# A convolution by transforms on one core: two products moved by a quarter of a row, and DRAM pitches off 4096 bytes

## The chip, the cores and the metric

The kernel runs on one core of a Trainium2 chip. The core has five engines that run side by side, each through its own list of instructions in order: PE (TensorE, matrix products; its weight loads are listed as PEld), DVE (VectorE), ACT (ScalarE), POOL (GpSimd) and SP (SyncE, which here only issues DMA transfers). POOL and ACT issue some transfers too. The transfers are carried by 16 DMA engines. Engines wait for each other with semaphores.

The metric is the device time of one execution in microseconds (us). The kernel before took 16473.95 us, the median of three runs (16464.4 to 16498.5).

## The reference

The input x has four images of 512 x 512 positions with 16 channels. Two layers follow each other, each with a group normalization in front and an addition of its own input behind:

```
x = x + conv_by_transform(gn(x), h0, numerators, denumerator)
x = x + cosine_conv_3x3(gn(x), kernel, bias, radius)
```

The first layer is a two-dimensional filter as long as the image. For each pair of an input and an output channel a rational function (numerator over denominator, 8 x 8 coefficients) gives a frequency response, from which a response of 512 x 512 taps is made. Each image, padded to 1024 x 1024, is transformed, multiplied at every frequency with the 16 x 16 matrix of that frequency, and transformed back; the first 512 x 512 positions are kept. The second layer is a 3 x 3 convolution divided by the norm of its window, with an arccosine and a hyperbolic tangent of the norms. All is in float32.

## The kernel before, in words

The work runs in four stages, one after the other.

- *filter_phase* makes the matrices of the frequencies along the width and stores them in the DRAM tensors g_d, four of them with 128 rows each. A row holds, for 128 places along the height, 16 output channels j with 8 x 16 numbers each: 8 KB per place.
- *forward_phase* transforms x along the width and stores it in x_d (four tensors, 128 rows of 256 KB).
- *conv_phase* takes one row, that is one frequency along the width, after the other: 513 steps of the same kind, since the first frequency is done in two. Within a row it transforms along the height, mixes the channels, and transforms back. The results go to y_d (four tensors, 128 rows of 256 KB).
- *last_phase* transforms y_d back along the width (the inverse), and then does the second layer.

The change is in conv_phase and in the pitches of g_d, x_d and y_d. A row n goes through conv_phase in five steps, so step(n) works on five rows at once:

- `load_x(n + 3)`, `load_g(n + 2)`, `load_xe(n + 1)`: SP issues the loads. x is 256 KB, g is 1 MB. xe comes in two transfers of 1.5 MB (line 814), read back from the small DRAM buffers xf_d in a shifted form.
- `turn_x(n + 3)` prepares the coefficients dfs_n of one row: one ACT instruction (763) and one DVE instruction (765).
- `x_part(n + 2, m)` for the four images m: the transform of x along the height, one product on PE per image (776, two matmuls each in the trace) into the PSUM tile px, which takes two images. After the second and the fourth, `evict` copies px into the first part of xe.
- `x_late(n + 2)`: POOL issues the store of xe to xf_d (790), multiplies xe with turning factors (four products in 797, then 798) and adds (799) to get xl, and stores xl (790). Behind it `half_shift` lets ACT copy one half of xe and one half of xl into another part of xe (808). The second of these copies needs xl.
- `g_part(n + 1, j)`: the transform of g along the height on PE (828), 16 channels j, into the PSUM tiles pg, and from there by `evict` into gh. There are three such tiles, and a quarter of a row takes two.
- `mix(n, g)`: the product over channels on PE (844), from xe and gh into pm, and from there by `evict` into yf.
- `over_q(n - 1, t)`: the first inverse step. PE transposes yf into pz (865), ACT copies one half out as zq (872), and DVE does five operations (873 to 877) that give z. After the last, POOL makes zd and z of it (881, 883).
- `over_g(n - 2, m)` for m from 0 to 3: the last inverse step on PE (902, four matmuls per m in the trace) from z and zd into the PSUM tile py. After m = 3 it is copied to yo, which POOL stores to y_d (913).

`evict` gives every third copy to DVE (726) and the others to ACT (728), in the order in which the program calls it. The tiles px, pz and py share three PSUM buffers. The tile xe has three buffers in SBUF; g, x, gh, yf and z have two each, and xl has one.

A step has four quarters, k = 0 to 3. Each does eight `mix` groups, four `g_part`, four `over_q`, and what the diff below shows. The calls only give the program order; the layer that records the program then places each engine's instructions, so the order on one engine may differ a little from that of the calls. SP's own order is x, xe, g, xe, in every row.

In g_d, x_d and y_d a row has PITCH floats added behind it. The helper `dram(t, row, offset, *dims)` builds the access: the row pitch comes from the tensor's shape, the rest from the call.

## Time and profile before

| what | value |
|---|---|
| median of three runs | 16473.95 us |
| the profiled execution's own time | 16489.29 us |
| its span in the profile | 16487.4 us |
| granted PE clock, mean | 0.972 |
| busy: PE, DVE, POOL, ACT | 91%, 64%, 62%, 54% of the span |
| DMA moved | 4542.92 MB, 276 GB/s on average |
| SP's queue (q1) | 67.9% of the time of 16 DMA engines |
| POOL's queue (q0) | 9.5% |
| stages, from the windows of the trace | filter to about 3560 us, forward to 4600, convolution to 13610, inverse to 14560, the rest to the end |

The page gives averages over stages of different kinds, so what a change in conv_phase is worth has to be read from that stage. A group of instructions has its line number, its engine, and the tiles that it writes and reads. In a list of waits "A <- B" says that A's engine stood idle until B released it; "issue" is a wait with no semaphore that the profile shows. A busy PE is not PE at its peak, because the ends of matmuls are modelled. An instruction of PE in float32 shows as two in the trace.

### The profile page before, as it was taken

Reading aid. Unit: us, or ns where it says so; the run is one execution under the profiler, and the core shown is the slowest. Engines: PE = TensorE matmul, PEld = TensorE weight load, DVE = VectorE, ACT = ScalarE, POOL = GpSimd, SP = SyncE. Lnnn points to the kernel's source line nnn. Section 1 sums busy time; section 2 is a strip of 40 time slices with the busy share of each in tenths; the row PEclk is TensorE's granted clock in tenths of the full one; section 3 lists DMA queues with packets and bytes.
Section 4 is the critical chain, followed back from the end, with each engine's and each line's share of the span. In section 5 each row is a group of like instructions: output and inputs, shape, how many; then the busy total and the mean of one; then the engine's idle time right before and its main releaser. Section 6 shows DMA issues by size and latency. Waiting matters only on the chain. (4 is left out here: it accounts for less than half of the span.)

```text
span 16487.4 us, 538106 instructions
## 1 busy us (share of the span) xinstructions
PE 15039.9 (91%) x232588; PEld 11221.5 (68%) x232588; DVE 10549.6 (64%) x20763; ACT 8870.6 (54%) x17007; POOL 10203.4 (62%) x9645
## 2 busy tenths in 40 slices
PE   7999999999988889898988899888889998988898
PEld 5555555554567777677777777777777777777787
DVE  8999999974545555555555555555555552447877
ACT  4666666653345555555555555555555551027888
POOL 7777777763356666666666666666666660237766
PEclk8999999999999999999999999999999999989999
DMA  4888888888888888888888888888888886885531
GB/s 139 241 244 247 240 243 248 240 244 250 251 282 328 324 326 330 317 327 329 328 329 317 326 328 327 317 318 324 324 326 329 326 321 232 313 279 167 167 110 67
DMA packets 2914640, 4542.92 MB, mean 276 GB/s; under 512 B 126114, under 2 KB 2094460, under 8 KB 2801422
## 3 DMA queue, kind: packets, MB, share of 16 engines
q1 hardware_dynamic: 2703070, 3836.37, 67.9%
q0 software_dynamic: 172336, 605.00, 9.5%
q10 hardware_dynamic: 36864, 67.13, 1.2%
q8 instruction: 1833, 30.03, 0.7%
q14 instruction: 537, 4.40, 0.1%
HBM read 3030.71 MB, written 1477.31 MB: 273 GB/s over the span
## 5 line engine op out<-in xcount | busy, mean ns | idle before, releaser
L828 PE MATMUL pg<-c_dg,g 64*128 64x128 f32 x32832 | 2838.7, 290 | 344.4 <-ACT gh L728 192.2
L844 PE MATMUL pm<-xe,gh 128*32 128x64 f32 x131328 | 2380.2, 222 | 520.0 <-issue 299.3
L844 PEld LDWEIGHTS pm<-xe,gh 128*32 128x32 f32 x131328 | 2001.1, 110 | 1113.6 <-issue 891.7
L828 PEld LDWEIGHTS pg<-c_dg,g 64*128 64x128 f32 x32832 | 2277.5, 189 | 690.3 <-issue 248.1
L873 DVE TENSOR_TENSOR z<-zq,pz 128x256 f32<-128x256 f32 x2052 | 859.5, 419 | 2634.6 <-ACT zq L872 2567.4
L726 DVE COPY gh<-pg 128x512 f32<-128x512 f32 x2046 | 1408.2, 688 | 1208.9 <-PE pg L828 1205.8
L458 PE MATMUL pt<-ev_in,c_todd 128*128 128x512 f32 x4096 | 1927.5, 609 | 16.2 <-DMA ev_in<-g_d 16.2
L797 POOL TENSOR_TENSOR xu<-xe,c_late 128x256 f32<-128x256 f32 x2052 | 1391.7, 702 | 808.5 <-ACT xe L728 791.2
L388 DVE RECIPROCAL dn<-dn 128x256 f32<-128x256 f32 x1024 | 1722.8, 1724 | 17.6
L728 ACT COPY yf<-pm 128x512 f32<-128x512 f32 x2046 | 1211.4, 592 | 886.9 <-PE pm L844 873.2
L389 POOL TENSOR_TENSOR sp<-m,dn 128x512 f32<-128x512 f32 x1024 | 1300.9, 1271 | 592.4 <-DVE dn L388 552.0
L808 ACT COPY xe<-xl 64x1024 f32<-64x1024 f32 x513 | 538.7, 1050 | 1877.9 <-POOL xl L799 1877.8
L728 ACT COPY gh<-pg 128x512 f32<-128x512 f32 x2058 | 1200.2, 583 | 368.8 <-PE pg L828 365.7
L865 PE MATMUL pz<-c_ident,yf 128*128 128x128 f32 x8208 | 1371.7, 290 | 24.2 <-issue 10.8
L458 PEld LDWEIGHTS pt<-ev_in,c_todd 128*128 128x128 f32 x4096 | 728.2, 190 | 920.6 <-issue 792.3
L417 ACT COPY st<-pg 128x256 f32<-128x256 f32 x2048 | 616.8, 391 | 1301.5 <-PE pg L406 1301.3
L406 PEld LDWEIGHTS pg<-c_dinv,sp 64*128 64x128 f32 x16384 | 1005.5, 196 | 442.2 <-ACT sp L394 232.6
L799 POOL TENSOR_TENSOR xl<-xl,xu 128x1024 f32<-128x1024 f32 x513 | 1209.5, 2358 | 40.2
L406 PE MATMUL pg<-c_dinv,sp 64*128 64x128 f32 x16384 | 1108.2, 287 | 60.2 <-ACT sp L394 44.6
L881 POOL TENSOR_TENSOR zd<-z 128x512 f32<-128x512 f32 x513 | 653.7, 1274 | 765.4 <-DVE z L873 765.3
L1279 PE MATMUL pc<-l_band,xn 128*128 128x160 f32 (+2 forms) x6144 | 1076.2, 333 | 51.7 <-DVE e_o L1334 51.7
L913 POOL DMA_DIRECT2D y_d<-yo x511 | 296.5, 580 | 1325.0 <-ACT yo L728 1299.8
(211 smaller groups left out, 30193.2 us busy)
## 6 DMA issues: line engine op xcount, KB each, us to landing
xe<-xf_d SPq DMA_DIRECT2D x1026, 1536.0 KB
g<-g_d SPq DMA_DIRECT2D x511, 1024.0 KB
g_d<-st SPq DMA_DIRECT2D x256, 1024.0 KB
ev_in<-g_d SPq DMA_DIRECT2D x1024, 256.0 KB
g_d<-ot SPq DMA_DIRECT2D x1024, 256.0 KB
xf_d<-xe POOLq DMA_DIRECT2D x513, 448.0 KB, 8.2
xf_d<-xl POOLq DMA_DIRECT2D x513, 448.0 KB, 5.4
x_d<-xo SPq DMA_DIRECT2D x128, 1024.0 KB
```

The costliest lines, as they stand in the source:

```text
L388: nc.vector.reciprocal(dn, dn)
L389: nc.gpsimd.tensor_mul(w["sp"][:, v], w["m"][:, v], bc(dn, 2, [P, 2, 2, P]))
L406: nc.tensor.matmul(pg[u][:, n, k].rearrange("p a x -> p (a x)"), w["sp"][q, n, k, c, :], dinv[q, 2 * kp + k, c, :], start=(c == 0), stop=( ...
L458: nc.tensor.matmul(pt, todd[:, c, kc, hh * P : hh * P + P], ev[:, kc, c], start=(kc == 0), stop=(kc == 1),)
L726: nc.vector.tensor_copy(dst, src)
L728: nc.scalar.copy(dst, src)
L797: nc.gpsimd.tensor_mul(u[:, :, h, c], xe[:, :, h, 1 - c], bc(late[:, 1 + c], 2, [P, F, 2]))
L799: nc.gpsimd.tensor_add(xl.rearrange("p f h c k -> p (f h c k)"), xl.rearrange("p f h c k -> p (f h c k)"), u.rearrange("p f h c k -> p (f ...
L828: nc.tensor.matmul(pg[c][:, j % 4], g[half, j], dg[half], start=True, stop=True)
L844: nc.tensor.matmul(pm[32 * q : 32 * q + 32, g % 8], gh[:, f].rearrange("p c j -> p (c j)"), xe[:, :, f].rearrange("p t h c k -> p t (h c k ...
L865: nc.tensor.transpose(pz[:, t % 4].rearrange("p v q x -> p (v q x)"), y[:, at].rearrange("p g x -> p (g x)"), ident)
L1279: nc.tensor.matmul(pc[:, lo:hi, :].rearrange("p w j -> p (w j)"), xns[q][:, h * P + dh : h * P + dh + P], bands[dh][:, o : o + hi - lo, :] ...
```

## The change

The order of the quarters changes in three places. `x_part` of two of the four images is called at the end of the fourth quarter of the step before, the other two stay at the end of the first quarter, ahead of `x_late`. `turn_x` is called in the second quarter instead of the third. `over_g` is called for two m in the second quarter and for two in the third, instead of for all four in the third.

The pitches change as well. A place of g takes 8 KB + 512 bytes (GP = 2176 floats) instead of 8 KB; G_ROW follows. PITCH goes from 1024 to 1152 floats, so that rows of g_d, x_d and y_d have 4.5 KB added instead of 4 KB. The places where g is stored (424), read back and stored (444, 464) and loaded (735, 738) follow the new pitch. The bytes that are moved and the length of each piece stay as they were.

```diff
+GP = C * 8 * C + 128
-G_ROW = 2 * S * C * 8 * C
+G_ROW = P * GP
-PITCH = 1024
+PITCH = 1152
...
-                            out=dram(g_d[h], None, a * G_ROW // 2 + ((32 * q + 16 * kp) * C + j) * 8 * C,
-                                     [C * 8 * C, 16], [1, 8 * C]),
+                            out=dram(g_d[h], None, a * G_ROW // 2 + (32 * q + 16 * kp) * GP + j * 8 * C,
+                                     [GP, 16], [1, 8 * C]),
...
-                return [((first[c] + 4 * (tb % 8)) * C + j) * 8 * C for c in range(2)]
-
-            step = [C * 8 * C, 4], [1, 8 * C]
+                return [(first[c] + 4 * (tb % 8)) * GP + j * 8 * C for c in range(2)]
+
+            step = [GP, 4], [1, 8 * C]
...
-                nc.sync.dma_start(out=t, in_=dram(g_d[rc], r, 0, [w, P], [1, w]))
+                nc.sync.dma_start(out=t, in_=dram(g_d[rc], r, 0, [GP, P], [1, w]))
...
-                    nc.sync.dma_start(out=t[to : to + 32], in_=dram(g_d[rc], r, at * w, [w, 32], [1, w]))
+                    nc.sync.dma_start(out=t[to : to + 32], in_=dram(g_d[rc], r, at * GP, [GP, 32], [1, w]))
...
                 if row(2) and k == 0:
-                    for m in range(B):
+                    for m in range(2, B):
                         x_part(n + 2, m)
                     x_late(n + 2)
                 if row(2) and k >= 2:
                     half_shift(n + 2, k - 2)
-                if row(3) and k == 2:
+                if row(3) and k == 1:
                     turn_x(n + 3)
-                if row(-2) and k == 2:
-                    for m in range(4):
-                        over_g(n - 2, m)
+                if row(3) and k == 3:
+                    for m in range(2):
+                        x_part(n + 3, m)
+                if row(-2) and k in (1, 2):
+                    for m in range(2):
+                        over_g(n - 2, 2 * (k - 1) + m)
```

## The prediction

> **What bounds the kernel now.** I read the page first (its chain of work that ended last is spread so thin over 538106 instructions that every entry rounds to 0%), then a table of busy time by stage. Columns: stretch in us, its length, busy us and instructions of PE, PEld, DVE, ACT and POOL, granted PE clock, share of the 16 DMA engines, GB/s.

> ```profile
> 0.00:3560.00 3560.00, 3475.22 (x29921) 2086.21 (x29922) 3328.98 (x3022) 2180.03 (x4860) 2636.11 (x2215) 0.98 0.80 231
> 4600.00:13610.00 9010.00, 8073.24 (x184035) 6436.62 (x184033) 4908.87 (x13272) 4771.32 (x8704) 5779.41 (x5639) 0.98 0.87 324
> 13610.00:14560.00 950.00, 841.16 (x4319) 725.11 (x4320) 335.09 (x928) 99.32 (x258) 142.49 (x64) 0.95 0.78 279
> ```

> The filter (first line) keeps PE busy 98% and hardly waits for DMA. The convolution (second) is 55% of the span; PE stands idle 10% of it, no engine is full, DMA is nearly so. The program order of its 513 rows repeats, so one row is the unit: from the first to the last row of the trace, 17.53 us each. Who waits there (us in total, times, longest, in 6000 to 13000 us, 400 rows):

> ```profile
> ACT xe L808 <- POOL xl L799: 1467.6, 399, 6.5
> PE pm L844 <- issue: 225.5, 225, 3.7
> PE pg L828 <- ACT gh L728: 152.9, 167, 3.8
> PE pm L844 <- DMA xe<-xf_d: 53.4, 50, 2.7
> ```

> ACT waits 3.7 us in every row for POOL's xl; the evictions of gh queue behind it, and PE behind those. The timeline of one row shows the loop (start, length, engine, line, operation):

> ```profile
> 6456.27 1.10 PE L844 MATMUL pm<-xe,gh 128*32 128x64 f32 x64 [0.39 <-ACT zq L872]
> ...
> 6460.60 1.36 POOL L797 TENSOR_TENSOR xu<-xe,c_late 128x256 f32<-128x256 f32 x2 [1.41 <-ACT xe L728]
> ...
> 6460.70 1.10 PE L844 MATMUL pm<-xe,gh 128*32 128x64 f32 x64
> ...
> 6461.10 0.68 DVE L726 COPY xe<-px 128x512 f32<-128x512 f32 x1
> ...
> 6462.08 0.56 POOL L790 DMA_DIRECT2D xf_d<-xe  x1
> ...
> 6466.02 2.36 POOL L799 TENSOR_TENSOR xl<-xl,xu 128x1024 f32<-128x1024 f32 x1
> ...
> 6468.41 1.06 ACT L808 COPY xe<-xl 64x1024 f32<-64x1024 f32 x1 [3.73 <-POOL xl L799]
> ...
> 6469.97 0.59 ACT L728 COPY gh<-pg 128x512 f32<-128x512 f32 x1
> ...
> 6470.62 1.16 PE L828 MATMUL pg<-c_dg,g 64*128 64x128 f32 x14 [1.08 <-ACT gh L728]
> ...
> 6472.38 0.68 DVE L726 COPY gh<-pg 128x512 f32<-128x512 f32 x1
> ...
> 6473.17 1.04 PE L844 MATMUL pm<-xe,gh 128*32 128x64 f32 x60 [0.39 <-ACT zq L872]
> ```

> Row to row it is 6473.17 - 6456.27 = 16.90 us. I count from T = 6460.70, the start of the second quarter (the end of x_part): xl is done at T+7.68, half_shift ends at 8.77, gh of the third quarter is out at 9.86, PE resumes at 9.92, the last gh is out at 12.36 (DVE first has five operations on z, released by ACT's zq), the next row's mix starts at 12.47 and its own second quarter 4.43 later: 16.90. In the trace 216 of 507 rows take up to 16.96 us; the others are longer, 0.63 on average over all. PE's own work without waits, summed from the usual length of each of its groups, is 14.96 us.

> Two things lengthen rows. One is PE "issue" stalls of about 1 us at no semaphore. The other is the load of xe (rows in which the mix starts 0.58 us after the last packet): by the trace's single packets this load ends 15.03 us (the median of 407 loads) after its issue, which in turn stands 5.42 us after xl is done (the store has to land).

> [...] gh and zq, long ready, stand 3.73 us behind L808. [...] POOL's stores and SP's loads share the time, at 87% here. [...] In 6000 to 13000 us there are 1131 packets of 16 KB on the instruction queue, 2.8 per row, and half of the PE gaps inside a group end within 1.45 us after one of them: not wholly hidden here.

> **The change part by part.** No instruction is added or removed. As built, POOL and SP keep their order; on PE two of four x_part products (4 of 8 matmuls in the trace) go from the end of the first quarter to the end of the fourth, before the next mix, and half of over_g goes from the third quarter to the second. DVE takes one yf in place of one gh. turn_x moves a quarter earlier: 0.52 us ACT and 0.55 us DVE, in slots where both wait (ACT idle 3.7 us); free, and without cover 0.5 us.

> *First quarter.* mix 1.03 + g 1.09 + transposes 0.59 + half x_part 0.91 = 3.62 us instead of 4.43 (before pulled one pair of g ahead of mix, after does not).

> *xl.* First-half xe is out before POOL has finished zd and z (they end near T-0.8), so POOL takes its first two products at once; it no longer idles 1.41. But the second half still comes at the end of the first quarter. DVE evicts it behind one z operation that waits for ACT's zq, near T-0.1: 0.25 to 0.93, against 0.40 to 1.08. POOL's store issue starts at 1.0 instead of 1.38; from there 6.30 to the end of xl (6468.38 - 6462.08): T+7.30. So 0.38 is won, not the whole 1.41.

> *The stall.* PE is in the fourth quarter at the same T as before: two quarters of 1.03 + 1.09 + 0.59 + 0.94 = 7.3. half_shift ends at 8.39, yf and gh bring 9.48, PE resumes at 9.54 (9.92 before); about 0.95 us of stall stays.

> *Into the next row.* g ends at 10.6, transposes 0.59, the moved half of x_part 0.91: PE is free at 12.1. zq at 9.76 lets DVE start; 1.6 for z, 0.68 for gh: 12.0. So mix starts near 12.15, and what was an idle gap and part of a stall now holds 0.91 of work. Row: 12.15 + 3.62 = 15.77 by engines alone. over_g's first half waits for DVE's eviction of px (0.93) and stands at 2.7: no wait. The moved x_part waits for yo (ACT, 10.25) and for x, issued a row earlier: none.

> *The load.* Issue at 7.30 + 5.42 = 12.72; plus 15.03 and 0.58: 28.33, which must equal 12.15 + one row: 16.18. Before, the same sum gives 7.68 + 5.42 + 15.61 - 12.47 = 16.24, hidden under 16.90; with the engines at 15.77 the load is the next thing late. Fast rows are then 16.2.

> *Stretching.* I keep 0.45 of the 0.63 for PE's own stalls (the rest I give to late loads), and add 0.10 since the spread of the load counts fully: 16.75. That is 0.78 per row, by 513 rows: -400 us.

> *Pitches.* All byte and packet counts stay. Packets of g take 345 ns on average (309 median), of xe, whose rows stand at 4.5 KB already, 177 (159): both 11% over, so a pitch off 4096 does not mark xe out. x stands at 85 (84), the 512-byte packets of the filter at 28.5 (27), and there PE hides them. I take 0. Ends: all of g's excess gone is 36 ns x 128 / 16 = 0.29 us of the load, -150 us; a loss of the same size is not excluded.

> The profiled execution took 16489.29 us (span 16487.4), 15 above the median of the runs shown. 16489 - 400 = 16089; on the median, **16074 us**.

> **Rivals.** *DMA holds more of it.* DMA works 0.87 x 17.53 = 15.2 us per row; at 16.75 that is 91%. If stores and loads now collide, the load grows by 0.4 and rows take 17.2: -170, 16300 us. For it: the share; against: the load kept to 15 us throughout. *The load is not in the way.* Shorter packets of g or earlier stores let the engine loop through: 15.8 + 0.45 = 16.25, -650, 15820 us. Against it: 16.18 above. *Slower.* Places 8.5 KB apart make g's reads slower, and these run between the two halves of xe's load. At 12.72 + L + 0.58 - 12.15 + 0.45 = 17.53 the load decides: L = 15.93, 0.9 us more, or 112 ns on each of g's packets. At half as long again (+173 ns, L = 16.4) it is +240 us, 16710. Against: the padded xe. *It doesn't do what it says:* if POOL still starts late, only x_part's place counts, rows near 16.9 to 17.5; that falls among the first rival or no change.

> **How the numbers follow.** Forecast 0.50 (15950 to 16200), DMA holds more 0.20 (16200 to 16430), load not in the way 0.17 (15750 to 15950), no change 0.04, slower 0.09. A measurement here tells about 0.2% from no change. Range 15820 to 16440 leaves about 2 in 10 out: half of the low case, no change and slower. Faster 0.87, same 0.04, slower 0.09.

> **What would show it.** In the convolution: rows near 16.2 at the fast end; POOL's wait for the first xe gone; ACT's wait at half_shift still above 2.5 us a row; PE's wait for gh in the fourth quarter near 1 us; more PE wait for DMA at mix; DMA share above 0.90; g packets near 345 ns; filter and inverse unmoved. It is wrong if fast rows stay at 16.9 (the loop is another), go to 15.8 (the load gave way), or if g's packets change by tens of ns.

## The result and the profile after

The changed kernel takes 16341.29 us, the median of four runs (16330.61 to 16345.83), against 16483.31 us for the kernel before on the same chip. The ratio is 0.9917, with a 95% interval of 0.9905 to 0.9930: faster by 0.83%. The forecast was 16074 us, so the change is faster as forecast, but by about 140 us and not 400.

The two profiled executions, cut at the same events, show where the time went (us):

| stretch | before | changed | difference |
|---|---|---|---|
| start to the first xl of the convolution | 4647.2 | 4634.0 | -13.2 |
| first to last xl, 512 rows | 8958.4 | 8868.0 | -90.4 |
| last xl to the first product of last_phase | 50.2 | 49.1 | -1.1 |
| from there to the last product of the inverse | 1040.7 | 1009.0 | -31.7 |
| the rest | 1791.0 | 1782.7 | -8.3 |
| span | 16487.4 | 16342.7 | -144.7 |

The convolution gave a quarter of what was forecast for it, and the other stages, on which the prediction put nothing, gave 54 us. Busy time by stage of the changed kernel (columns as before: stretch, length, busy us and instructions of PE, PEld, DVE, ACT and POOL, granted clock, DMA share, GB/s):

```profile
0.00:3560.00 3560.00, 3475.01 (x29916) 2086.05 (x29920) 3328.81 (x3021) 2179.47 (x4858) 2635.99 (x2215) 0.98 0.78 231
4600.00:13500.00 8900.00, 7905.48 (x183845) 6187.87 (x183845) 4751.66 (x13262) 4663.58 (x8697) 5735.58 (x5636) 0.98 0.87 328
13500.00:14450.00 950.00, 853.42 (x4550) 736.10 (x4547) 346.33 (x962) 103.34 (x266) 153.04 (x69) 0.96 0.79 289
```

In the convolution PE now stands idle 11% of the time, where it stood idle 10%; the DMA share is 0.87 as before and not above 0.90. The waits of the changed kernel in 6000 to 13000 us (405 rows; us in total, times, longest):

```profile
ACT xe L809 <- POOL xl L800: 1494.2, 405, 6.5
...
POOL xf_d L791 <- DVE zq L875: 659.1, 398, 5.2
...
PE pm L845 <- issue: 232.1, 195, 2.6
PE pm L845 <- DMA xe<-xf_d: 202.9, 128, 2.8
...
PE pg L829 <- ACT gh L729: 156.0, 179, 3.7
```

ACT still waits 3.7 us in every row for xl. PE's wait for the load of xe went from 53 us to 203. POOL no longer waits for the first half of xe; it waits for the second instead, to store it (that wait is listed with "DVE zq", the operation behind DVE's copy of that half). The timeline of one fast row (start, length, engine, line, operation):

```profile
9383.00 1.10 PE L845 MATMUL pm<-xe,gh 128*32 128x64 f32 x64
...
9385.80 1.36 POOL L798 TENSOR_TENSOR xu<-xe,c_late 128x256 f32<-128x256 f32 x2
...
9386.58 1.10 PE L845 MATMUL pm<-xe,gh 128*32 128x64 f32 x64
...
9387.01 0.68 DVE L727 COPY xe<-px 128x512 f32<-128x512 f32 x1
...
9387.99 0.56 POOL L791 DMA_DIRECT2D xf_d<-xe  x1 [0.83 <-DVE zq L875]
...
9391.91 2.36 POOL L800 TENSOR_TENSOR xl<-xl,xu 128x1024 f32<-128x1024 f32 x1
...
9394.30 1.05 ACT L809 COPY xe<-xl 64x1024 f32<-64x1024 f32 x1 [3.71 <-POOL xl L800]
...
9395.85 0.59 ACT L729 COPY gh<-pg 128x512 f32<-128x512 f32 x1
...
9396.13 0.43 PE L845 MATMUL pm<-xe,gh 128*32 128x64 f32 x15 [1.19 <-issue]
...
9399.05 1.10 PE L845 MATMUL pm<-xe,gh 128*32 128x64 f32 x64
...
9399.26 0.37 SPq L815 DMA_DIRECT2D xe<-xf_d  x1
```

From mix to mix this row takes 9399.05 - 9383.00 = 16.05 us, and its first quarter 3.58. The row also holds a gap of 1.19 us at "issue" in the mix of its fourth quarter, and does not get longer by it: PE's next work, a g_part, needs the tile that ACT empties into gh, and that copy ends at 9396.44, so PE would have waited anyway. The fast rows did fall, by 0.8 us where 0.7 was forecast. But only the fast rows did: a twentieth of the 512 rows took at most 16.88 us before and takes at most 16.07 now, the median went from 17.07 to 17.01, and the mean from 17.50 to 17.32. So the question is what stretches the rows.

### The profile page after: what moved, and what is told of

The parts are those of the page before. It is cut to its first block, busy times and chain, and to the rows that moved or that the text cites. A ratio compares the mean times of both kernels' runs of the same rounds, so it can differ in the third digit from the quotient of the medians.

```text
span 16342.7 us, 538107 instructions
## 1 busy us (share of the span) xinstructions
PE 14869.0 (91%) x232588; PEld 10969.0 (67%) x232588; DVE 10396.8 (64%) x20763; ACT 8766.8 (54%) x17007; POOL 10169.4 (62%) x9645
## 5 line engine op out<-in xcount | busy, mean ns | idle before, releaser
L829 PE MATMUL pg<-c_dg,g 64*128 64x128 f32 x32832 | 2599.4, 289 | 308.3 <-ACT gh L729 192.5
L829 PEld LDWEIGHTS pg<-c_dg,g 64*128 64x128 f32 x32832 | 2134.2, 190 | 573.3 <-ACT gh L729 245.9
L729 ACT COPY gh<-pg 128x512 f32<-128x512 f32 x2567 | 1446.9, 585 | 1296.4 <-PE pg L829 1293.9
L727 DVE COPY gh<-pg 128x512 f32<-128x512 f32 x1537 | 1056.7, 688 | 663.5 <-PE pg L829 660.3
L903 PE MATMUL py<-z,c_ig 128*64 128x256 f32 x6156 | 1127.4, 397 | 6.6 <-issue 2.2
L777 PE MATMUL px<-dfs_n,x 128*128 128x256 f32 x4104 | 1080.4, 387 | 12.7 <-DMA c_late<-k_late 11.5
```

The costliest lines, as they stand in the source:

```text
L729: nc.scalar.copy(dst, src)
L777: nc.tensor.matmul(px[:, b % 2].rearrange("p f c -> p (f c)"), state["x", n][:, b], state["dfs", n], start=True, stop=True)
L829: nc.tensor.matmul(pg[c][:, j % 4], g[half, j], dg[half], start=True, stop=True)
L903: nc.tensor.matmul(py[64 * half : 64 * half + 64, odd], ig[:, s0, c2], zs.rearrange("p (t h) j -> p h t j", h=2), start=(c2 == 0), stop=(c ...
```

## The experiments

Four theories appear in the expectations by letter, besides those that an expectation spells out. A: the pitches do nothing in the convolution, and what holds the rows there is xl, the landing of its store, the load of xe that waits for it, and the mix; B: the new places of g take part of the gain back. D: the DMA engines' throughput holds the rows, at 15.2 us of transfers a row. F: PE waits for its own instructions. R: POOL's xl, ACT's half_shift, the evictions behind it, and PE form a ring that sets the row.

For the kernels that bear on the rows of the convolution the table gives, in us a row, the length that a twentieth of the 512 rows do not exceed ("fast"), the mean of all 512, and two sums over PE's gaps of more than 0.45 us in 6000 to 13000 us (to 12800 for the last kernel). The first has the gaps that end 1.15 to 1.65 us after a packet of the instruction queue has ended; gaps spread evenly would fall there 8 times in 100. The second has all other such gaps. The last column is the time a row in which the trace grants PE half its clock. All are worked out from the trace's single packets, instructions and clock records.

| kernel | fast | mean | gaps after an instruction packet | other gaps | at half clock |
|---|---|---|---|---|---|
| before | 16.88 | 17.50 | 1.07 | 0.48 | 0.50 |
| changed | 16.07 | 17.32 | 0.89 | 0.91 | 0.53 |
| new order, old pitches | 16.07 | 17.29 | 0.91 | 0.93 | 0.52 |
| new pitches, old order | 16.89 | 17.48 | 0.88 | 0.62 | 0.47 |
| before, xe from the row before | 16.89 | 17.29 | 0.83 | 0.45 | 0.40 |
| changed, xe from the row before | 16.06 | 16.94 | 1.05 | 0.37 | 0.54 |
| changed, no loads of g | 16.03 | 16.94 | 1.41 | 0.16 | 0.55 |
| changed, store of xl on SP's queue | 16.37 | 17.37 | 0.96 | 1.06 | 0.30 |
| changed, store of xl on ACT's queue | 16.51 | 17.23 | 0.96 | 0.76 | 0.49 |
| all of x's transform in the fourth quarter | 20.56 | 20.81 | 1.23 | 2.36 | 4.20 |
| the same, half_shift on POOL | 14.92 | 17.16 | 1.44 | 0.26 | 0.87 |
| changed, half_shift on POOL | 14.98 | 17.36 | 1.14 | 0.79 | 1.03 |
| fourth quarter, POOL, an eighth of mix's products | 14.56 | 16.07 | 0.01 | 1.06 | 0.97 |

The last column belongs to the gaps. In 6000 to 13000 us the traces of before and of the changed kernel have 50 and 59 stretches at half clock, each of 3.41 us or a multiple of it. Each comes right behind 3.41 us in which PE was idle for at least 1.49 us (before) and 1.03 us (changed): 2.03 and 2.05 us on average, where an average 3.41 us have 0.35 and 0.37. In such a stretch of the changed kernel one matmul of mix takes 314 ns (the median), and 219 outside; 64 of them in a row start over 1.62 us, and over 0.88 outside (medians of 8 and 1365 cases). What rows lose at half clock is therefore put below at half of the last column, an estimate. That the stalls bring the clock down is read from this order in time; no run tests it alone. If they do, stalls that lie close together cost more than their own length.

### The two halves of the change

*The new order with the old pitches.*

```diff
-GP = C * 8 * C + 128
+GP = C * 8 * C
-PITCH = 1152
+PITCH = 1024
```

> The new order of the quarters with the old pitches (GP = 8 KB, PITCH = 1024). Theory A, late landing: the engines' loop became shorter as forecast, but the store of xl now meets the load of xe that is still under way, lands about 1 us later than I took (6.4 us in the profile of after against 5.4), and the transfers' loop holds the rows; the pitches do nothing. Then this is as fast as after: 16341 us, within 25. Rival B, pitches: reads of g at 8.5 KB places are slower (370 ns a packet against 345) and ate the gain of the order. Then this is at 16000 to 16150 us.

It took 16395.1 us: 0.9952 of before (0.9939 to 0.9964). That is 29 us above the range of theory A, and far from that of B.

*The new pitches with the old order*, which is the change without its edits in `step`.

> The new pitches with the old order. Theory A: no change from before, 16483 us within 30. Rival B: slower by what the pitches eat, 16630 to 16830 us.

It took 16432.05 us: 0.9975 of before (0.9963 to 0.9986), 21 us below the range of A, and on the other side from B. So the order gives 79 us against 16474.13 us for before on the same chip, and the pitches 42. The two together are 121 of the 142 us of the change; with the new order, and across two sets of runs, the pitches give 54. In the convolution the pitches give next to nothing: mean rows of 17.48 against 17.50 with the old order, 17.32 against 17.29 with the new. Theory B falls: g's packets took 362 ns with the new order and the old places, 351 with the old order and the new places, 370 with both, so their growth from 345 goes mostly with the order. What the pitches give lies outside the convolution, and is taken up below.

### Is the load of xe, or the transfers as a whole, in the way?

*The changed kernel with xe loaded from the buffer of the row before*, so that no load waits for a store that was just issued (xe then has parts of another row).

```diff
-            src = xf_d[n % 4]
+            src = xf_d[max(n - 1, 0) % 4]
```

> After, but xe is loaded from the DRAM buffer of the row before, so the load waits for no store of its own row (the values are the wrong row's; bytes, transfers and all other work are the same). Theory A: with the landing out of the loop rows fall to the engines' 16.1 us plus stalls of PE, 16.3 to 16.7 in the mean: 15800 to 16050 us. Rival D, throughput: the DMA engines' time per row (15.2 us at 87%) is the limit whatever the order; rows stay near 17.3 and the run at 16250 to 16400. Rival C, engines: the stretched rows are stalls of PE and not of transfers; also 16300.

*The changed kernel without the loads of g after the first rows* (later rows use the g of those).

```diff
+            if n > 3:
+                state["g", n] = kept[n % 2]
+                return
```

> After without the loads of g from the fifth row on (every row then uses the g of its parity's first whole row; 1 MB of 5.6 MB per row is left out, all other work is the same). Theory A: the load of xe ends about 2.5 us sooner after its issue, the transfers no longer hold the rows, 16.3 to 16.7 us in the mean: 15800 to 16050 us. Rival D expects the same here (15.2 us of DMA become 12.5). Rival C: rows stay at 17.3, 16300 us.

*The kernel before, with xe from the row before.* The edit is the same.

> The kernel before with xe loaded from the xf_d of the row before, so that no load waits for a store that has just been issued (the output is not the reference's). Theory A: before, the load held the mix by only 0.1 to 0.2 us a row (53 us in 400 rows): 16380 to 16450 us, with rows at the 16.9 us floor that the engines set; the changed kernel gained 187 us from the same edit. Theory F: rows stay 0.4 us above that floor, by PE's instruction fetches. If the load were before's real bound, it would fall under 16300.

The first took 16153.65 us and the second 16153.92, both 187 us less than the changed kernel; the third took 16377.72, 79 less than before (16457.06). The first two fall between the ranges of theory A and of its rivals; the third lies just under A's range, and its mean row stands 0.40 us above its fast row, as theory F had it. So the late load costs 0.38 us a row in the changed kernel (17.32 - 16.94) and 0.21 before. That is theory A in kind. But in size it is not the whole: with the load out of the way, rows go from 16.06 to a mean of 16.94. And without g, 13.0 us of transfers a row in place of 15.2 and a DMA share of 0.76 in the window, the mean is 16.94 all the same, so theory D does not explain what is left in these rows. What is left in both is mostly gaps after instruction packets, 1.05 and 1.41 us a row.

### Can the store be made to land earlier?

*The second store of x_late issued from SP's queue, and from ACT's, in place of POOL's* (`(nc.gpsimd, nc.sync)[half].dma_start(...)` in `store`).

> The changed kernel with the second store of x_late (xl to xf_d) issued from SP's queue, not from POOL's; nothing else moves. Theory A: the store's landing decides; if SP's queue lands it in 4.5 us instead of 6.4 to 6.7, about half of the 0.5 us a row that PE waits at the mix goes: 16150 to 16250 us. Theory D or F alone: 16320 to 16360 us, as the changed kernel.

> The changed kernel with the second store of x_late issued from ACT's queue. ACT then waits for xl to issue the store, as it already does for the half shift behind it. Theory A: as with SP's queue, 16150 to 16250 us, unless the earlier wait holds back ACT's evictions of g's products (then 16350 or more). Theories D and F: 16320 to 16360 us.

On SP's queue: 16374.78 us, 0.9944 of before (0.9924 to 0.9964), slower than the changed kernel by 33 and outside both ranges. The expectation's "if" did not hold: from the end of xl to the issue of the load it took 7.50 us on average instead of 6.41, and the load itself 16.90 instead of 15.38. On ACT's queue: 16295.11 us in one run, 46 less than the changed kernel. There the store's last packet comes 5.47 us after xl, but the load is issued only 6.1 us after it (6.6 in the changed kernel and 7.6 with SP's queue, when read in the same way). PE's waits for the load fall from 203 us to 69; but the fast rows rise from 16.07 to 16.51, and most of the gain is lost again.

### What the ring costs

*All four parts of x's transform, and x_late, at the end of the fourth quarter.*

```diff
-                if row(2) and k == 0:
-                    for m in range(2, B):
-                        x_part(n + 2, m)
-                    x_late(n + 2)
...
                 if row(3) and k == 3:
-                    for m in range(2):
+                    for m in range(B):
                         x_part(n + 3, m)
+                    x_late(n + 3)
```

> The changed kernel with all four parts of x's transform (of row n+3), not half of them, and x_late behind them at the end of the fourth quarter: xl is finished about one first quarter (3.5 us) earlier in the row. Theory A (the row is the loop xl, landing of its store, load of xe, mix; the landing is 6.4 to 6.7 us and not 5.4): PE's wait for the load at the mix (203 us in 400 rows) is gone, as in the run that loads the row before (16153.7 us), so 16100 to 16180 us. Theory F (what is left is PE waiting for its own instructions, about 0.9 us a row, on top of PE's own work, 15.4 us a row): ACT's wait for xl at the half shift goes too, so the fast row falls under 16.0 us and the mean to about 16.4: 15850 to 16000 us. Theory D (the 16 queues' throughput, 15.2 us of transfers a row, is what remains): no better than the changed kernel by more than 50 us, 16290 or more.

It took 18130.97 us: 1.1007 of before (1.0988 to 1.1026). No theory foresaw that; D's "16290 or more" holds, but not for D's reason, since the DMA share fell to 0.72. The timeline shows why:

```profile
9008.94 1.10 PE L845 MATMUL pm<-xe,gh 128*32 128x64 f32 x64
...
9013.56 2.37 POOL L800 TENSOR_TENSOR xl<-xl,xu 128x1024 f32<-128x1024 f32 x1
...
9015.96 1.04 ACT L809 COPY xe<-xl 64x1024 f32<-64x1024 f32 x1 [5.80 <-POOL xl L800]
...
9017.51 0.59 ACT L729 COPY gh<-pg 128x512 f32<-128x512 f32 x1
...
9018.15 1.69 PE L829 MATMUL pg<-c_dg,g 64*128 64x128 f32 x14 [2.35 <-ACT gh L729]
```

In the recorded order ACT has the second half_shift right behind the first quarter's work, not where `step` calls it: the layer that records the program had moved it ahead together with x_late. ACT waits 5.80 us there, the gh behind it is late, and PE waits 2.35 us for that. In the changed kernel the same wait begins a quarter later in PE's work, and so costs less. The clock adds to it: 4.20 us of each row run at half clock, where the changed kernel has 0.53.

*The same kernel, with that copy on POOL, right behind xl.*

```diff
-            nc.scalar.copy(
+            (nc.scalar.copy, nc.gpsimd.tensor_copy)[half](
```

> All four parts of x's transform at the end of the fourth quarter (the kernel that took 18131), and the second half_shift (xl into xe) copied by POOL, right behind xl, not by ACT. Theory R (the row is the ring POOL's xl, ACT's half_shift, the evictions queued behind it on ACT, PE): the ring is cut, ACT waits for xl no longer, and xl is ready a first quarter (3.5 us) earlier, so neither ACT nor the load of xe is late. What is left is PE's own work (15.0 us a row without waits) and its instruction fetches (0.9): fast rows 15.2 to 15.7 us, a mean of 16.2 to 16.6, 15750 to 15950 us. Theory D (transfers, 15.2 us a row of the 16 queues, already hold the changed kernel): no better than 16250. If POOL itself is the ring (its store of y waits for ACT's yo, and xl stands behind it): rows stay above 17.3 us, 16340 or more.

*The changed kernel with that copy on POOL.*

> The changed kernel with the second half_shift copied by POOL; x's transform stays where the change put it. Theory R: ACT's wait for xl (1494 us in 405 rows) is gone and with it PE's at gh; but xl is done at the same time, so the load of xe holds two rows: 7.3 + 6.6 (landing) + 15.1 (load) + 0.6 + 3.6 = 33.2 us, 16.6 a row, and with a part of the fetches 16.9 to 17.2: 16120 to 16280 us. Theory D: 16300 to 16360.

The first took 16268.18 us: 0.9869 of before (0.9856 to 0.9883). It is 73 us faster than the changed kernel and the fastest of the kernels here that do all the work. Against 18131, one copy of 1 us on another engine is worth 1863 us: the ring of theory R set the rows there. Of the 3.65 us by which the mean row fell, 1.67 is, by that estimate, what PE no longer loses at half clock (half of 4.20 - 0.87). The fast rows are 14.92 us, PE's own work and shorter than forecast. But the time lies outside R's range: the mean is 17.16 and not 16.2 to 16.6. It is in fact what theory D had, "no better than 16250", so this run leaves D open; the run under "What 'issue' is" settles it. The waits of this kernel in the same window say what is left:

```profile
PE pm L846 <- issue: 433.0, 357, 3.1
...
PE pg L830 <- issue: 140.2, 105, 2.7
...
PE pg L830 <- DMA g<-g_d: 80.5, 64, 2.3
...
PE pm L846 <- DMA xe<-xf_d: 26.3, 26, 4.2
```

ACT's wait for xl is gone, and so is PE's for gh. Waits for the load of xe came down to 26 us. The stalls at "issue" nearly doubled, from 232 us to 433 at the mix. With no wait for other engines left to hide them, the parts add up: 1.44 + 0.26 us of gaps and an estimated 0.44 for the half clock make 2.14 of the 2.24 us by which the mean row exceeds the fast one.

The second took 16378.92 us, 0.9941 of before (0.9926 to 0.9957), 38 us slower than the changed kernel and above the ranges of both R and D. Its fast rows fell from 16.07 to 14.98, so the ring had set the fast rows of the changed kernel too; but xl is ready as late as there, and PE now waits 345 us for the load of xe at the mix. Cutting the ring alone moves the wait to the load.

### What "issue" is

*The kernel of 16268 us, with the mix of eight groups done as one product of 512 columns* (seven of eight groups get the weights of the first, so the result is another; the columns that go through PE, the evictions and the transfers stay).

```diff
-            for q in range(4):
-                f = g + 32 * q
+            for q in range(4) if g % 8 == 7 else ():
+                f = g - 7 + 32 * q
...
-                    xe[:, :, f].rearrange("p t h c k -> p t (h c k)"), start=True, stop=True,
+                    xe[:, :, f : f + 8].rearrange("p t f h c k -> p t (f h c k)"), start=True, stop=True,
```

> The kernel with all of x's transform in the fourth quarter and POOL's half_shift (16268 us, fast rows of 14.97, mean 17.19), with the mix done by one product of 512 columns for eight groups instead of eight products of 64: the same columns go through PE, the same transfers run, but PE has 248 products a row instead of 360 (the weights of seven groups in eight are left out, so the result is another). Theory F (PE waits for its own instructions): its stalls after a packet of the instruction queue fall from 1.76 us a row by at least the share of the instructions, to 1.2 or less, and the mean row to 16.6 or less: 15970 us or less. Theory D (the 16 queues carry 15.1 us of transfers in every row): the mean row stays above 17.0, 16170 us or more.

It took 15718.39 us: 0.9529 of before (0.9511 to 0.9546), 550 us less than the kernel it was made from. The count in the expectation was too small, since the trace lists two matmuls for each product in float32: it lists 136 a row in place of 360. The mix on the page, in the kernel of 16268 us and in this one (busy, mean ns, idle before it):

```profile
L846 PE MATMUL pm<-xe,gh 128*32 128x64 f32 x131328 | 2431.8, 223 | 586.7 <-issue 546.5
```

```profile
L846 PE MATMUL pm<-xe,gh 128*32 128x512 f32 x16416 | 2264.4, 625 | 105.0 <-DMA xe<-xf_d 79.6
```

The mix's own work fell by 7%, and its 547 us of idle time at "issue" have gone. The instruction queue in 6000 to 12800 us (packets, MB, share of the DMA engines), again first the one, then the other:

```profile
q8 instruction: 1119, 18.33, 1.0%
```

```profile
q8 instruction: 454, 7.44, 0.4%
```

Of 1152 packets in 6000 to 13000 us of the first kernel 441 were followed by a gap, 1.33 us each; of the 454 here 4 were. The DMA share rose from 0.88 to 0.93 and the mean row fell to 16.07, so the transfers had room, and theory D falls for the kernel of 16268 us. The edit takes out weight loads along with products, so by itself it does not name the fetch; the timing does. Of the 521 gaps in the first kernel 441 end 1.15 to 1.65 us after an instruction packet, 85% where chance gives 8. The two together show theory F: the stalls at "issue" are mostly PE waiting for its own instructions. Part of the 550 us is a faster row besides (14.92 to 14.56, some 185 us); the stretch above the fast row fell from 2.24 to 1.51 us. In this kernel PE waits for g's load instead (384 us at pg), which points to the transfers of theory D as the next thing late.

### Where the pitches' 42 us come from

Seven kernels with the old order. Four give the new pitch to some of g_d, x_d and y_d; three put unused tensors between these, with the old pitches or with y_d's new one. The edits are of these forms:

```diff
-    y_d = [tc.dram_tile([P, Y_ROW + PITCH], F32, name=f"y_d{r}") for r in range(4)]
+    y_d = [tc.dram_tile([P, Y_ROW + 1152], F32, name=f"y_d{r}") for r in range(4)]
...
+    gap = tc.dram_tile([P, 4 * 16512], F32, name="gap")
```

> The kernel before with only the rows of y_d at the new pitch (1152 floats added, not 1024); g_d, x_d and the order as before. If the inverse stage's gain of 32 us (1041 us to 1009) comes from the pitch of y_d, which that stage reads across rows: 16430 to 16450 us, and the inverse stage near 1009. If it comes from what the change does to g_d or x_d (where they and their neighbours then lie): 16465 to 16480, the inverse stage at 1041.

> The kernel before with g_d alone in its new form (places of 8.5 KB, rows with 1152 floats added); x_d, y_d and the order as before. If the pitches' gain comes from g_d: 16425 to 16445 us, of it 32 in the inverse stage, which never touches g_d and so can only gain from where the tensors behind g_d then lie. If it needs x_d's pitch: 16465 to 16485.

> The kernel before with all pitches as before, and behind g_d a tensor of 33.8 MB that nothing uses but one small transfer at the start: what lies behind g_d is moved by as much as the change moves it. If the inverse stage gains from where its tensors lie: 16435 to 16455 us, the inverse stage near 1009 us; if from g_d's places themselves: 16465 to 16490 and 1041.

> The kernel before with the rows of x_d and y_d at the new pitch, g_d as before. If the inverse stage's gain comes from x_d's pitch, or from y_d's with what lies behind it moved by x_d's growth: the inverse stage near 1009 us, 16440 in all. If it needs g_d's growth as well: 1041 to 1046 us, 16465 to 16485.

> The kernel before with all pitches as before and two unused stretches of DRAM, one behind g_d as large as the growth of g_d and x_d, one behind y_d as large as the growth of y_d: what the inverse stage reads and writes starts where the change puts it. If the places decide: the inverse stage near 1009 us. If the pitch of y_d is needed too: 1041 to 1046 us.

> The kernel before with x_d alone at the new pitch. If the shift of everything behind x_d by its growth (4 x 64 KB) is enough: the inverse stage near 1005 us, 16430 to 16450 in all. If y_d's pitch is needed with it: 1041 to 1046 us, 16465 to 16490.

> The kernel before with y_d alone at the new pitch and an unused stretch of DRAM of 256 KB ahead of it, as large as the growth of x_d. If the gain is y_d's pitch at another place: the inverse stage near 1005 us. If it needs the pitch of x_d itself: 1041 to 1046 us.

| new pitch of | unused DRAM | time, us | before beside it, us | to the first xl | inverse stage | 512-byte packets there, ns |
|---|---|---|---|---|---|---|
| none (before) | | | | 4647.2 | 1040.7 | 37.0 |
| g, x, y | | 16432.05 | 16474.13 | 4637.9 | 1009.0 | 31.0 |
| y | | 16482.28 | 16474.86 | 4647.6 | 1046.5 | 38.7 |
| g | | 16473.43 | 16494.46 | 4638.1 | 1042.0 | 36.6 |
| none | behind g | 16478.69 | 16494.46 | 4648.0 | 1044.2 | 36.7 |
| x, y | | 16412.49 | 16485.49 | 4646.3 | 1004.4 | 31.1 |
| none | behind g, behind y | 16470.26 | 16485.49 | 4648.5 | 1042.8 | 37.8 |
| x | | 16428.86 | 16466.56 | 4647.8 | 1010.1 | 30.9 |
| y | ahead of y | 16481.04 | 16466.56 | 4645.7 | 1037.8 | 36.0 |

The last four are single runs, each beside one of before. The ratios for the three others are 1.0004 (0.9997 to 1.0011) for y alone, 0.9991 (0.9983 to 0.9999) for g alone, and 1.0000 (0.9991 to 1.0008) with DRAM left free behind g. Two things are clear. g's new places bring the start of the convolution 9 us forward, with or without the others; that is the end of the filter, where g is read back. And the inverse stage is 30 to 36 us shorter in each kernel in which x_d has the new pitch, and at most 3 us shorter in the others, though this stage neither reads nor writes x_d. So the expectations that laid the gain on y_d's pitch, on g_d or on the places alone failed. In the kernels with the shorter stage the 512-byte packets of that stage take 31 ns on average instead of 36 to 39; they are the reads of yw_d, which the inverse writes and the preparation of the last stage reads back beside it. The waits in the inverse stage, of the kernel before and then of the changed one:

```profile
DVE l_stats L1067 <- POOL p_x L1071: 195.7, 48, 11.9
...
PE po L1141 <- DVE yo L1149: 67.1, 23, 6.2
```

```profile
DVE l_stats L1071 <- POOL p_x L1075: 163.0, 48, 13.4
...
PE po L1145 <- DVE yo L1153: 49.4, 22, 5.4
```

DVE waits 33 us less for POOL's additions, which take those reads in, and PE 18 us less for DVE. That the shorter packets bring this about is likely from these lines, but not shown. Why x_d's pitch does that stays open: where the tensors lie in DRAM was not seen, and the shifts tried by unused tensors did nothing.

## Why the prediction was right or wrong, point by point

**First quarter: right.** 3.62 us forecast, 3.58 in the fast row.

**xl: wrong by 0.39 us.** POOL did take its first two products at once (T - 0.78 with T = 9386.58), and its wait for the first half of xe is gone. But its store of xe needs the second half. DVE copies that from T+0.43 to T+1.11, later than the 0.25 to 0.93 forecast, since the first z operation waits 1.79 us for ACT's zq; and the store starts at T+1.41, not at 1.0, with a release that the trace puts at another operation of DVE. xl is done at T+7.69, against 7.68 before and 7.30 forecast. half_shift, the last evictions and the next mix are late by about the same: the mix at T+12.47, not 12.15. The engines' row is 16.05 us where 15.77 was worked out.

**The load: right in kind, its size wrong twice.** The landing was taken from one fast row, 5.42 us. Over all rows it was 5.57 before and 6.41 now (median 6.68). That the stores meet more of the loads fits this: without g's loads the load of xe is issued 4.0 us after xl on average, where it is 6.6 in the changed kernel. And the sum was closed over one row, with the next mix fixed at 12.15, where the loop passes through two: (7.69 + 6.41 + 15.38 + 0.58 + 3.58) / 2 = 16.8 us a row with the measured values, and 16.7 before. So the fast rows, at 16.07, are not held by the load as forecast (16.2), but many others are: loading the row before saves 0.38 us a row.

**Stretching: the step that failed.** The prediction kept 0.45 us of PE's own stalls and added 0.10. Measured: 0.87 us without the load's part (16.94 - 16.07), and 1.25 with it. The 0.63 of before was read as if it were all there was. It was the part of PE's stalls that stuck out of other waits. The gaps after instruction packets alone came to 1.07 us a row before, in rows that even at their fastest held 1.9 us of waiting (16.88 against 14.96 of PE's own work), so that more than half of them cost nothing. With the load of xe out of the way on both sides it is plainest: 0.83 us of such gaps lengthened the rows of before by 0.40, and 1.05 those of the changed kernel by 0.88. Taking waiting time out of the row did not take those stalls out; it uncovered them. The time lost at half clock, half of 0.50 and of 0.53 us a row by the estimate above, is much the same before and now, 0.25 and 0.27, so it is not what changed. In the sum: stretching 0.42 more than kept, load 0.28 more than given, fast row 0.13 better; 0.57 us by 513 rows is 292 us of the 310 that the convolution fell short. The rest is the mean row of before, 17.50 over all rows where 17.53 was used.

**Pitches: wrong outside the convolution.** In the convolution zero was right, and so was the sentence that nothing marks xe out. But 9 us at the end of the filter and 32 us in the inverse stage were put at nothing; the ends of 150 us, worked out for g's loads, had no part in it. x_d's rows are 256 KB and had 4 KB added before; here another 512 bytes on them are worth 30 us, in a stage that does not touch x_d (1010.1 us with x_d's new pitch alone, 1040.7 before).

**The signs named.** Right: POOL's wait for the first xe gone, ACT's wait at half_shift above 2.5 us (3.7), more wait for the load at mix. PE's wait for gh came to 0.87 us where it occurred, near the 1 us named, but in 179 of 405 rows at most; in the row shown a gap at "issue" took its place. Nearly right: fast rows 16.07 instead of 16.2. Wrong: DMA share 0.87, not above 0.90, because the mean row hardly fell; g's packets 370 ns on average instead of 345 (the median stayed at 309, and the load of xe grew only from 15.11 to 15.38 us), a change of tens of ns that the prediction had named as a sign of being wrong, though it goes mostly with the order and not with the pitch; filter and inverse moved.

**The rivals.** Rows of 17.2 were worked out for the rival "DMA holds more of it", near the 17.32 measured, but the reason is only in part the right one: the late load is 0.38 us of the row, and without g's loads the mean row falls no further than without the landing. The slower rival did not occur; g's reads are slower on average by 25 ns, not 112. PE's gaps after packets of the instruction queue were named in the prediction, and then given no rival of their own. That was the mistake.

## What to carry to other kernels

A stall that lies inside another wait is not priced by how far it sticks out: before a wait is taken away, add up the stalls that it hides, here PE's gaps after packets of the instruction queue, and expect more of them to show: 0.40 of 0.83 us a row before and 0.88 of 1.05 in the changed kernel, once the load of xe was out of the way. A loop through a store and a load that reads it back is closed over as many rows as it spans, with the landing averaged over all rows, not taken from a fast one. A copy that waits for another engine can be issued by that engine: it stands behind its producer there, and holds nobody else's queue. That was worth 1863 us where xl came early, and cost 38 where the load of xe became the next thing late.

## What the runs showed of the hardware

In the changed kernel 25% of the packets of the instruction queue, 16 KB each, were followed by a gap of PE (291 of 1142, 1.24 us each). In the kernel of 16268 us, whose other gaps came to only 0.26 us a row, 38% were (441 of 1152, 1.33 us). Both have about 2.8 packets a row. With the mix as one product of 512 columns, at 1.1 packets a row, 4 of 454 were. No run lies between these two rates.

Without g's loads, at a DMA share of 0.76, the stalls were longer than with them (1.42 us against 1.24) and 408 in the window, so they need no full DMA engines.

A copy of 64 x 1024 floats from xl to xe took POOL 1.03 us and ACT 1.05.
